# A message-passing layer with gathers on two engines: seven instead of eight one-hot tiles a pair of chunks

## The chip, the core and the metric

The kernel runs on one core of one Trainium2 chip. The metric is device time in microseconds, median of the runs; lower is better. TensorE is called PE, VectorE DVE, ScalarE ACT, GpSimd POOL and SyncE SP.

## The reference

A graph has 12500 nodes with 32 features and 400000 edges, sorted by destination. Each edge makes a value from both of its nodes and its own 32 features; each node takes the maximum over its incoming edges.

```python
h = jnp.maximum(_layernorm(x, axis=-1), 0.0)
e_feat = jnp.concatenate([h[src], h[dst], edge_attr], axis=-1)
v = jax.nn.relu(e_feat @ W1 + b1) @ W2 + b2          # (400000, 96) -> 64 -> 32
x_cand = jax.ops.segment_max(v, dst, num_segments=12500)
out = x + jnp.maximum(x_cand, h)
```

## The kernel before

The edges are cut into four stripes of 100352, and each stripe into 196 chunks of 512; a chunk `c` means 512 edges of every stripe, 2048 edges, whose 32 features times four stripes fill the 128 partitions. The main loop takes a pair of chunks a turn (`for c in range(0, NCH - 4, 2)`, with `a, b = c + 2, c + 3` the pair after the one that is being finished). 94 of its turns are alike.

The rows `h[src]` of a chunk are 16 groups of 128 edges. They come in two ways:

- **Gathered rows.** POOL issues one indirect DMA for each group of 128 rows (`gather`, line 179), three groups to a buffer `gh`. `HELD` holds some of these gathers until TensorE has reached a named point of an earlier turn (`b1` is the odd chunk's tile 1, `n0` the next even chunk's tile 0, `ea` the edge features, `ht` the gathered features, `tr` the transposes, `lv` the windows' maxima), so that POOL runs beside TensorE at a set distance.
- **Rows by matmuls, called tiles.** In chunks 2 to 193 the last `MM = 4` groups are picked out of `hs`, the whole of `h` in SBUF, by one-hot matrices (`tile`, line 344): seven slices `hot[:, k]` of 128x128 for 128 edges, each against the high and the low half of `hs`, 14 matmuls into one PSUM bank of 32 features times 14. DVE then multiplies by a mask over the 14 (`one`, line 351) and takes the maximum (line 352), which leaves one row of 32 features for each edge. In 34 of the odd chunks (`MMX`) a fifth group goes this way; its one-hots (line 274), mask and keys are made and loaded by `one_hot_x` and `load_key_x`.

The one-hots of a chunk compare `keys` (which group of 14 nodes a source belongs to) with the slice's numbers: DVE makes slices 0 to 3 in two instructions of two slices (`one_hots`, line 304), ACT slices 4 to 6 (`one_hots_act`, lines 317 and 318).

DVE turns gathered rows and tiles' rows into features by edges (`to_features`, lines 368 and 371). TensorE adds the edge features (`ea`), the destination's part (`of`, `qf`) and the gathered features (`ht`) into four banks `ph` (line 773), ACT applies the ReLU (line 798), TensorE multiplies by W2 (line 807), DVE runs a maximum along the edges (`scan`, line 815), and the last edge of each node is picked by transposes (line 669) and one-hot matmuls (line 686), for which DVE makes `last` (line 650). SP writes the windows to `top_d` (line 707).

The order on every engine is the order in which the program is written out (a manual schedule). In one turn TensorE does: `ea`, `of`, `ht`, the transposes, tiles 1 to 3 of the even chunk, the second layer, the windows' maxima, tiles 0 to 3 of the odd chunk, its fifth where there is one, and tile 0 of the next even chunk. Seven PSUM banks go round. `PAD` and its like only place buffers.

Of the kernel before, what the change touches and what calls it, by code (L numbers as in the profile page):

```python
# [8 lines left out]
F32 = mybir.dt.float32  # L9
# [15 lines left out]
P = 128  # L25
# [24 lines left out]
MMC = range(2, NCH - 2)  # L50
MMX = [17 + 2 * (k * 83 // 34) for k in range(34)]
RAW = 2
TILES = len(MMC) * MM
PLACES = TILES + len(MMX)
SLOTS = 48
PAD = 16
PAD_HOT = 24
# [19 lines left out]


def ap(t, offset, dims):
    return bass.AP(tensor=t.tensor, offset=t.offset + offset, ap=dims)  # L80


@with_exitstack
def gnn_kernel(ctx, tc, x, src, src_mm, src_x, src_t, dst, dst_ext, lo, lo_c, ends_b, edge_attr, weights, w1, w2, b2, out):

# [26 lines left out]
    top_d = dram.tile([NP, D], F32, name="top_d")  # L112
    key_d = dram.tile([(TILES + len(MMX)) * P], F16, name="key_d")
    acc_d = dram.tile([NP, D], F32, name="acc_d")
# [35 lines left out]
    place_k = const.tile([P, TILES + SLOTS], F32, name="place_k")[:, :PLACES]  # L150
    src_xi = const.tile([P, SLOTS], I32, name="src_xi")[:, :len(MMX)]
    nc.sync.dma_start(src_xi, src_x)

# [17 lines left out]


    def gather(c):
        n = min(K - MM * (c in MMC), (SE - c * C) // D) - (c in MMX)
        parts = []
        for k in range(0, n, SOME):
            parts.append(gathered.tile([P, SOME, D], F32, name="gh"))
            for i in range(min(SOME, n - k)):
                ins = nc.gpsimd.indirect_dma_start(  # L179
                    out=parts[-1][:, i, :], out_offset=None, in_=h_d[:, :],  # L180
                    in_offset=bass.IndirectOffsetOnAxis(ap=src_i[:, c, k + i:k + i + 1], axis=0))
                hold(c, k + i, ins)
        return parts
# [57 lines left out]
    def places(start, stop):  # L241

        se = src_i[:, MMC.start + start:MMC.start + stop, K - MM:]
        pk = place_k[:, :len(MMC) * MM].rearrange("p (c m) -> p c m", m=MM)[:, start:stop]
        group(pk, se)
        nc.vector.scalar_tensor_tensor(pk, pk, -float(A0), se, op0=ALU.mult, op1=ALU.add)

    extras = {}

    def places_x():  # L250

        pk = place_k[:, TILES:]
        group(pk, src_xi)
        nc.vector.scalar_tensor_tensor(pk, pk, -float(A0), src_xi, op0=ALU.mult, op1=ALU.add)

    def load_key_x(c):

        if c in MMX:
            small = early.tile([P, P // 2 + A0], F32, name="kx", bufs=2)
            key = small[:, :P // 2].bitcast(F16)  # L260
            nc.scalar.dma_start(key, ap(key_d, (TILES + MMX.index(c)) * P, [[0, P], [1, P]]))
            extras[c] = key, small[:, P // 2:], []

    def one_hot_x(c):

        if c in MMX:
            key, mask, spaces = extras[c]
            for k in range(0, A1, 2):
                if k:
                    spaces.append(early.tile([P, HALF, D], F32R, name="xg", bufs=3).rearrange("p k d -> p (k d)"))  # L270
                else:
                    spaces.append(early.tile([P, ZERO], F32R, name="zero", bufs=1)[:, :2 * P])
                n = min(2, A1 - k)
                nc.vector.tensor_tensor(spaces[-1].rearrange("p (k e) -> p k e", k=2)[:, :n],
                                        key[:, None, :].to_broadcast([P, n, P]),
                                        key_ps[:, k:k + n, None].to_broadcast([P, n, P]), op=ALU.is_equal)
            i = TILES + MMX.index(c)
            nc.vector.tensor_tensor(mask, place_ps, place_k[:, i:i + 1].to_broadcast([P, A0]), op=ALU.is_equal)

    def load_keys(c, queue=nc.scalar):  # L280

        if c in MMC and (c - MMC.start) % KEYS == 0:
            n = min(KEYS, MMC.stop - c)
            kb = early.tile([P, KEYS, MM * P], F16, name="kb", bufs=2)
            queue.dma_start(kb[:, :n], ap(key_d, (c - MMC.start) * MM * P,
                                           [[0, P], [MM * P, n], [1, MM * P]]))
            for k in range(n):
                keys[c + k] = kb[:, k]

# [7 lines left out]
    def one_hots(c, start, stop):  # L297

        if c not in MMC:
            return  # L300
        n = stop - start
        if n == 0:
            return
        nc.vector.tensor_tensor(hot_of(c)[:, start:stop], keys[c][:, None, :].to_broadcast([P, n, MM * P]),  # L304
                                key_ps[:, start:stop, None].to_broadcast([P, n, MM * P]), op=ALU.is_equal)

# [4 lines left out]
    def one_hots_act(c):  # L311

        if c not in MMC:
            return
        for k in by_act(c):
            away = early.tile([P, MM * P], F32, name="away", bufs=2)
            nc.scalar.activation(away, keys[c], AF.Square, bias=key_n[:, k:k + 1])  # L317
            nc.scalar.activation(hot_of(c)[:, k], away, AF.Relu, bias=ones, scale=-1.0)  # L318

    def mask_of(c):  # L320
        if c in MMC:
            masks[c] = early.tile([P, MM, A0], F32, name="mask", bufs=2)
            nc.vector.tensor_tensor(
                masks[c], place_ps[:, None, :].to_broadcast([P, MM, A0]),
                place_k[:, (c - MMC.start) * MM:(c - MMC.start + 1) * MM, None].to_broadcast([P, MM, A0]),
                op=ALU.is_equal)

    def tile(c, m):

        if c not in MMC or m == MM and c not in MMX:  # L330
            return
        if m == 0:
            mm_rows[c] = early.tile([P, MM, D], F32, name="gm", bufs=4)
        if m < MM:
            hot = [hots[c][:, k, m * P:(m + 1) * P] for k in range(A1)]
            mask, row = masks[c][:, m], mm_rows[c][:, m]
        else:
            _, mask, spaces = extras.pop(c)
            hot = [spaces[k // 2][:, k % 2 * P:(k % 2 + 1) * P] for k in range(A1)]
            row = gh[c][-1][:, SOME - 1]  # L340
        po = bank("pv")[:, :D * A0]
# [14 lines left out]
    def to_features(c, part):  # L356
# [6 lines left out]
        ht = hts[c]  # L363
        n = min(K - MM * (c in MMC), (SE - c * C) // D)
        if part < J:
            r = slice(part * SOME, min((part + 1) * SOME, n))
            if r.start < n:
                nc.vector.transpose(ht[:, r].rearrange("p k e -> p (k e)"),  # L368
                                    gh[c][part][:, :r.stop - r.start].rearrange("p k f -> p (k f)"))
        elif c in MMC:  # L370
            nc.vector.transpose(ht[:, n:].rearrange("p k e -> p (k e)"),
                                mm_rows.pop(c).rearrange("p k f -> p (k f)"))
        else:
            for k in range(J, len(gh[c])):
                r = slice(k * SOME, min((k + 1) * SOME, n))
                nc.vector.transpose(ht[:, r].rearrange("p k e -> p (k e)"),
                                    gh[c][k][:, :r.stop - r.start].rearrange("p k f -> p (k f)"))
# [35 lines left out]
    with tc.tile_pool(name="nodes", bufs=1) as pool, tc.tile_pool(name="nodes_ps", bufs=2, space=PSUM) as ps:  # L413
        sp = pool.tile([P, TILES + len(MMX)], I32, name="sp")
        nc.scalar.dma_start(sp, src_mm)
# [107 lines left out]
        for k in range(2):  # L523
            split_1(k)
            q_transpose(k)
        key = pool.tile([P, TILES + len(MMX)], F32, name="key")
        key16 = pool.tile([P, TILES + len(MMX)], F16, name="key16")
        group(key, sp, key16)
# [34 lines left out]
    with tc.tile_pool(name="edges", bufs=3) as pool, tc.tile_pool(name="edges_ps", bufs=1, space=PSUM) as ps:  # L563
# [290 lines left out]
        for c in range(0, NCH - 4, 2):  # L854
# [42 lines left out]
            load_keys(a + KEYS)  # L897
            load_key_x(b + 2)
            if c:
# [34 lines left out]
            if c == 2 * AHEAD:  # L934
                places(FIRST, len(MMC))
                places_x()
            if (c + 4) % BLOCK == 0 and (c + 4) // BLOCK < NB:
# [10 lines left out]
            if c:  # L948
                tile(b, 3)
            tile(b, MM)  # L950
            to_features(b, 3)
# [235 lines left out]
```

## Time and profile before

| | |
|---|---|
| median of 3 runs | 3579.48 us (3571.26 to 3581.6) |
| the profiled execution | 3575.96 us, its span 3574.1 us |
| granted TensorE clock | 0.944 |
| busy: PE, PEld, DVE, ACT, POOL | 3241.7, 2547.7, 2223.2, 1578.5, 2207.4 us |
| one-hot matmuls (line 344), busy | 2373.0 us in the largest of three groups |
| gathers (line 179) | 2291, 2169.8 us busy |

A row of a group reads: line, engine, operation, out<-in by tile names, shape, count, busy time in us and mean ns of one, and behind the second bar the idle time of the engine just ahead of these instructions, with what ended it ("issue" is a wait for nothing that the profile shows; "remote" one whose releaser it does not know). PEld is TensorE's loading of weights, which overlaps its matmuls. In a timeline a row reads: start, duration, engine, line, operation, tiles, count, and in brackets the idle time ahead. Ends of matmuls are modelled in this profile.

### The profile page before, as it was taken

To read this page: it belongs to the slowest core of one execution; us is meant where nothing else is said; L and a number is where in the kernel's file an instruction comes from. 1 tells how busy PE (TensorE), PEld (TensorE's weight loads), DVE (VectorE), ACT (ScalarE), POOL (GpSimd) and SP (SyncE) were. 2 spreads that over 40 slices of the span, in tenths; PEclk is the share of its full clock that TensorE was granted. 3 is DMA by queue.
4 is the path that set the end of the run, shared out by engine and by line. 5 is a ranking of instruction groups with operands and counts; after the bars stand their busy time and mean duration, and the time that the engine had idled before them with its cause. 6 is when DMAs were issued, how large, how long until landed. Compare 5 with 4: busy or idle time off the path is not lost.

```text
span 3574.1 us, 55458 instructions
## 1 busy us (share of the span) xinstructions
PE 3241.7 (91%) x19141; PEld 2547.7 (71%) x19141; DVE 2223.2 (62%) x4215; ACT 1578.5 (44%) x2470; POOL 2207.4 (62%) x2337
## 2 busy tenths in 40 slices
PE   5899999989999998999999999989999999999987
PEld 3577777777777776777777767777777777777765
DVE  5456666666666666666666666656665666666655
ACT  3344444443534444444443434444444444444443
POOL 6666666665666666666666666666666666666662
PEclk8899999999999999999999999999999999999997
DMA  5322222222222222222222222222222222222222
GB/s 175 99 60 62 53 64 62 62 50 62 64 62 53 61 63 65 50 66 60 62 50 70 57 56 58 59 59 61 60 62 59 60 61 61 63 65 49 59 58 65
DMA packets 178819, 227.49 MB, mean 64 GB/s; under 512 B 109621, under 2 KB 150373, under 8 KB 165734
## 3 DMA queue, kind: packets, MB, share of 16 engines
q10 hardware_dynamic: 29828, 108.01, 9.6%
q0 software_dynamic: 74336, 38.21, 8.5%
q1 hardware_dynamic: 74370, 77.70, 7.0%
q8 instruction: 151, 2.47, 0.3%
q14 instruction: 134, 1.10, 0.1%
HBM read 212.23 MB, written 11.46 MB: 63 GB/s over the span
## 4 chain that ended last, share of the span: by engine, by line
PE 81%; issue 10%; DVE 6%; another core or an unknown queue 2%; SPq 1%; DMA 1%; ACT 1%; DVEq 0%; ACTq 0%
PE pv L344 60%; PE ph L773 10%; PE pv L686 4%; PE pv L669 3%; PE pv L807 3%; DVE hot L304 1%; DVE one L351 1%; DVE last L650 1%; DVE sm L815 1%; DMA top_d<-wo 0%; DVE ht L368 0%; SPq L616 0%; SPq L707 0%; SPq L625 0%
## 5 line engine op out<-in xcount | busy, mean ns | idle before, releaser
L179 POOL DMA_INDIRECT gh<-h_d,src_i x2291 | 2169.8, 947 | 1296.3 <-issue 560.0
L344 PE MATMUL pv<-hs,hot 128*128 128x448 f32 x10752 | 2373.0, 378 | 97.5 <-issue 83.9
L344 PEld LDWEIGHTS pv<-hs,hot 128*128 128x128 f32 x10752 | 2089.1, 196 | 345.7 <-issue 159.7
L351 DVE TENSOR_TENSOR one<-pv,mask 128x448 f32<-128x448 f32 x768 | 472.3, 615 | 1219.7 <-remote 464.7
L798 ACT ACTIVATE hid<-ph,wt 128x512 f32<-128x512 f32 x392 | 250.0, 688 | 1124.6 <-remote 498.2
L352 DVE TENSOR_REDUCE gm<-one 128x32 f32<-128x448 f32 x768 | 476.2, 620 | 26.5
L304 DVE TENSOR_TENSOR hot<-kb,consts 128x1024 fp32r<-128x1024 f16 (+1 forms) x379 | 447.5, 1199 | 0.0
L318 ACT ACTIVATE hot<-away,ones 128x512 fp32r<-128x512 f32 x582 | 421.6, 724 | 45.0 <-remote 26.1
L317 ACT ACTIVATE away<-kb,key_n 128x512 f32<-128x512 f16 x582 | 416.0, 715 | 0.0
L692 ACT ACTIVATE wo<-pv 128x256 f32<-128x256 f32 x95 | 36.6, 385 | 631.2 <-remote 439.2
L815 DVE TENSOR_TENSOR_SCAN sm<-pb,sm,pv 128x512 f32<-128x512 bf16 x195 | 243.6, 1249 | 16.5 <-remote 9.0
L686 PEld LDWEIGHTS pv<-so,last 128*128 128x128 f32 x768 | 107.5, 191 | 159.5 <-issue 148.5
L773 PE MATMUL ph<-ht,wt 32*64 32x512 f32 x1568 | 197.3, 618 | 21.0 <-issue 13.0
L686 PE MATMUL pv<-so,last 128*128 128x256 f32 x768 | 148.6, 304 | 74.3 <-issue 67.7
L368 DVE STREAM_TRANSPOSE ht<-gh 128x96 f32<-128x96 f32 x774 | 207.4, 269 | 1.2
L661 ACT ACTIVATE sb<-sm,wt 128x512 f32<-128x512 f32 x196 | 138.1, 715 | 138.7 <-issue 87.6
L669 PEld LDWEIGHTS pv<-ident,sb 128*128 128x128 f32 x782 | 91.8, 150 | 120.3 <-issue 95.1
L773 PE MATMUL ph<-of,qf 32*64 32x512 f32 x1552 | 147.6, 600 | 19.6 <-issue 17.5
L669 PE MATMUL pv<-ident,sb 128*128 128x128 f32 x782 | 126.4, 298 | 30.4 <-issue 24.4
L773 PEld LDWEIGHTS ph<-ht,wt 32*64 32x64 f32 x1568 | 62.7, 135 | 114.1 <-issue 98.5
L642 ACT ACTIVATE of<-of,ones 128x512 f32<-128x512 f32 x194 | 140.6, 725 | 6.3
L641 ACT ACTIVATE of<-db,below 128x512 f32<-128x512 int32 x194 | 137.4, 708 | 0.0
(115 smaller groups left out, 1328.2 us busy)
## 6 DMA issues: line engine op xcount, KB each, us to landing
ea<-in_edge_attr SPq DMA_DIRECT2D x49, 1024.0 KB
db<-in_dst_ext ACTq DMA_DIRECT2D x48, 1024.0 KB
gh<-h_d,src_i POOLq DMA_INDIRECT x2291
pb<-pen_d ACTq DMA_DIRECT2D x48, 512.0 KB
kb<-key_d ACTq DMA_DIRECT2D x47, 512.0 KB
top_d<-wo SPq DMA_DIRECT2D x752, 3.0 KB
qf<-q_d SPq DMA_DIRECT2D x392, 16.0 KB
q_d<-qs SPq DMA_DIRECT2D x6, 512.0 KB
```

What stands on the lines that cost most here:

```text
L179: ins = nc.gpsimd.indirect_dma_start(out=parts[-1][:, i, :], out_offset=None, in_=h_d[:, :], in_offset=bass.IndirectOffsetOnAxis(ap=src_i[ ...
L304: nc.vector.tensor_tensor(hot_of(c)[:, start:stop], keys[c][:, None, :].to_broadcast([P, n, MM * P]), key_ps[:, start:stop, None].to_broad ...
L317: nc.scalar.activation(away, keys[c], AF.Square, bias=key_n[:, k:k + 1])
L318: nc.scalar.activation(hot_of(c)[:, k], away, AF.Relu, bias=ones, scale=-1.0)
L344: ins = nc.tensor.matmul(po, hot[k], hs[:, part, k].rearrange("p f a -> p (f a)"), start=(k == 0 and part == 0), stop=(k == A1 - 1 and par ...
L351: nc.vector.tensor_tensor(one, of_group, mask[:, None, :].to_broadcast([P, D, A0]), op=ALU.mult)
L352: nc.vector.tensor_reduce(row, one, axis=AX.X, op=ALU.max)
L669: passes(c // 2 + 1, "tr", nc.tensor.transpose(px[:, j, :], sb[:, j * P:(j + 1) * P], ident))
L686: ins = nc.tensor.matmul(pw[:, x % n], last[x][:, j].rearrange("p s w -> p (s w)"), sos[x][0][:, j], start=(j == 0 and x < n), stop=(j == ...
L773: ins = nc.tensor.matmul(ph[s][x * HID:(x + 1) * HID], w[g], e[g], start=start, stop=stop)
L798: nc.scalar.activation(hid[k], of, AF.Relu, bias=b1c)
L815: nc.vector.tensor_tensor_scan(found[:, :n], loaded.pop(c)[2][:, :n], pv[:, :n], -LOW if before is None else before[:, C - 1:C], op0=ALU.a ...
```

## The change

Even chunks keep four tiles; odd chunks have three, and the fifths of 34 odd chunks are gone, so a pair has seven tiles. Odd chunks gather 13 groups instead of 12 or 11; their last buffer holds four groups (`gl`, two buffers), and the buffers of three are 13 instead of 14. The fifths' keys, one-hots, masks and loads go. The one-hots, masks and keys of odd chunks shrink to three groups. `HELD` is written anew for 25 gathers a pair, with 11 points instead of 12 (there is no `b3` any more).

```diff
-MMX = [17 + 2 * (k * 83 // 34) for k in range(34)]
...
-HELD = {0: (3, 'b1'), 2: (3, 'b2'), 4: (3, 'b3'), 6: (3, 'n0'), 8: (2, 'ea'), 10: (2, 'ht'), 12: (2, 'tr'), 14: (2, 'a1'), 16: (2, 'a2'), 18: (2, 'a3'), 20: (2, 'lv'), 22: (2, 'b0')}
+HELD = {0: (3, 'b1'), 2: (3, 'b2'), 5: (3, 'n0'), 8: (2, 'ea'), 10: (2, 'ht'), 12: (2, 'tr'), 14: (2, 'a1'), 16: (2, 'a2'), 19: (2, 'a3'), 22: (2, 'lv'), 24: (2, 'b0')}
...
+def tiles_of(c):
+    return MM - c % 2 if c in MMC else 0
...
-    gathered = ctx.enter_context(tc.tile_pool(name="gathered", bufs=14))
+    gathered = ctx.enter_context(tc.tile_pool(name="gathered", bufs=13))
...
+    def rows_in(c):
+
+        n = min(K - tiles_of(c), (SE - c * C) // D)
+        at = list(range(0, n, SOME)) + [n]
+        if len(at) > 2 and at[-1] - at[-2] == 1:
+            del at[-2]
+        return [slice(k, m) for k, m in zip(at, at[1:])]
+
     def gather(c):
-        n = min(K - MM * (c in MMC), (SE - c * C) // D) - (c in MMX)
         parts = []
-        for k in range(0, n, SOME):
-            parts.append(gathered.tile([P, SOME, D], F32, name="gh"))
-            for i in range(min(SOME, n - k)):
+        for r in rows_in(c):
+            if r.stop - r.start > SOME:
+                parts.append(gathered.tile([P, SOME + 1, D], F32, name="gl", bufs=2))
+            else:
+                parts.append(gathered.tile([P, SOME, D], F32, name="gh"))
...
-        nc.vector.tensor_tensor(hot_of(c)[:, start:stop], keys[c][:, None, :].to_broadcast([P, n, MM * P]),
-                                key_ps[:, start:stop, None].to_broadcast([P, n, MM * P]), op=ALU.is_equal)
+        w = tiles_of(c) * P
+        nc.vector.tensor_tensor(hot_of(c)[:, start:stop, :w], keys[c][:, None, :].to_broadcast([P, n, w]),
+                                key_ps[:, start:stop, None].to_broadcast([P, n, w]), op=ALU.is_equal)
...
-        if c not in MMC or m == MM and c not in MMX:
+        if m >= tiles_of(c):
             return
...
-            load_key_x(b + 2)
...
-            one_hot_x(b)
...
-            tile(b, MM)
```

On TensorE, one turn of the main loop with a fifth tile, from the edge features on, stood in this order before (L344 are tiles; `zero` and `xg` hold the fifth's one-hots):

```order
L773 MATMUL ph<-ea,wt 64x512 x8
L773 MATMUL ph<-of,qf 64x512 x8
L773 MATMUL ph<-ht,wt 64x512 x8
L669 MATMUL pv<-ident,sb 128x128 x8
L344 MATMUL pv<-hs,hot 128x448 x42
L807 MATMUL pv<-hid,wt 32x512 x8
L686 MATMUL pv<-so,last 128x256 x8
L344 MATMUL pv<-hs,hot 128x448 x56
L344 MATMUL pv<-hs,zero 128x448 x4
L344 MATMUL pv<-hs,xg 128x448 x10
L344 MATMUL pv<-hs,hot 128x448 x14
```

The same turn now, with line numbers of the changed kernel:

```order
L758 MATMUL ph<-ea,wt 64x512 x8
L758 MATMUL ph<-of,qf 64x512 x8
L758 MATMUL ph<-ht,wt 64x512 x8
L654 MATMUL pv<-ident,sb 128x128 x8
L328 MATMUL pv<-hs,hot 128x448 x42
L792 MATMUL pv<-hid,wt 32x512 x8
L671 MATMUL pv<-so,last 128x256 x8
L328 MATMUL pv<-hs,hot 128x448 x56
```

Between the windows' maxima (`so`, `last`) and the next edge features stood six tiles, or five in a turn without a fifth; now there are four (56 matmuls), three of the odd chunk and the next even chunk's first.

On DVE, the part of a turn from the odd chunk's second tile to its third stood so before, in a turn with a fifth tile (`hot` is the second half of DVE's one-hots of the next even chunk):

```order
L351 TENSOR_TENSOR one<-pv,mask 128x448
L352 TENSOR_REDUCE gm<-one 128x32
L368 STREAM_TRANSPOSE ht<-gh 128x96
L650 TENSOR_TENSOR last<-consts,at 128x512 x2
L304 TENSOR_TENSOR hot<-kb,consts 128x1024
L323 TENSOR_TENSOR mask<-consts,place_k 128x56
L274 TENSOR_TENSOR zero<-kx,consts 128x256
L274 TENSOR_TENSOR xg<-kx,consts 128x256 x2
L274 TENSOR_TENSOR xg<-kx,consts 128x128
L278 TENSOR_TENSOR kx<-consts,place_k 128x14
```

It now stands so, and runs on to the end of the odd chunk:

```order
L335 TENSOR_TENSOR one<-pv,mask 128x448
L336 TENSOR_REDUCE gm<-one 128x32
L353 STREAM_TRANSPOSE ht<-gh 128x96
L635 TENSOR_TENSOR last<-consts,at 128x512 x2
L291 TENSOR_TENSOR hot<-kb,consts 128x1024
L312 TENSOR_TENSOR mask<-consts,place_k 128x56
L335 TENSOR_TENSOR one<-pv,mask 128x448
L336 TENSOR_REDUCE gm<-one 128x32
L353 STREAM_TRANSPOSE ht<-gh 128x96
L353 STREAM_TRANSPOSE ht<-gl 128x128
L356 STREAM_TRANSPOSE ht<-gm 128x96
```

The fifth's five instructions are gone from behind the mask. What stands ahead of the one-hots is the same as before; the odd chunk's third tile is now its last, and its last gathered buffer has four groups.

More of the change, by code (lines that the diff above doesn't have):

```diff
@@ L50 @@
 MMC = range(2, NCH - 2)
-MMX = [17 + 2 * (k * 83 // 34) for k in range(34)]
 RAW = 2
[L53 to L56, printed above, removed]
+TILES = sum(MM - c % 2 for c in MMC)
+PAD = 48
 PAD_HOT = 24
@@ L76, with first_of @@
 EPS = 1e-5
+def tiles_of(c):
+    return MM - c % 2 if c in MMC else 0
+def first_of(c):
+    return sum(tiles_of(k) for k in range(MMC.start, c))
 def ap(t, offset, dims):
@@ L112, in gnn_kernel @@
     top_d = dram.tile([NP, D], F32, name="top_d")
-    key_d = dram.tile([(TILES + len(MMX)) * P], F16, name="key_d")
+    key_d = dram.tile([TILES * P], F16, name="key_d")
     acc_d = dram.tile([NP, D], F32, name="acc_d")
@@ L170, in gnn_kernel @@
     general_i = const.tile([1, 1], I32, name="general_i")
+    def rows_in(c):
[4 more added lines that the diff above has]
+        return [slice(k, m) for k, m in zip(at, at[1:])]
     def gather(c):
-        n = min(K - MM * (c in MMC), (SE - c * C) // D) - (c in MMX)
         parts = []
-        for k in range(0, n, SOME):
-            parts.append(gathered.tile([P, SOME, D], F32, name="gh"))
-            for i in range(min(SOME, n - k)):
+        for r in rows_in(c):
[3 more added lines that the diff above has]
+                parts.append(gathered.tile([P, SOME, D], F32, name="gh"))
+            k = r.start
+            for i in range(r.stop - r.start):
                 ins = nc.gpsimd.indirect_dma_start(
@@ L241, in places @@
     def places(start, stop):
[L243 to L278, printed above, removed]
+        pairs = place_k.rearrange("p (c m) -> p c m", m=2 * MM - 1)[:, start // 2:stop // 2]
+        for x in range(2):
+            n = MM - x
+            se = src_i[:, MMC.start:MMC.stop].rearrange("p (c x) t -> p c x t", x=2)[:, start // 2:stop // 2, x, K - n:]
+            pk = pairs[:, :, x * MM:x * MM + n]
+            group(pk, se)
+            nc.vector.scalar_tensor_tensor(pk, pk, -float(A0), se, op0=ALU.mult, op1=ALU.add)
     def load_keys(c, queue=nc.scalar):
@@ L284, in load_keys @@
             kb = early.tile([P, KEYS, MM * P], F16, name="kb", bufs=2)
-            queue.dma_start(kb[:, :n], ap(key_d, (c - MMC.start) * MM * P,
-                                           [[0, P], [MM * P, n], [1, MM * P]]))
+            flat = kb.rearrange("p k e -> p (k e)")
+            at = [(first_of(k) - first_of(c)) * P for k in range(c, c + n + 1)]
+            queue.dma_start(flat[:, :at[n]], ap(key_d, first_of(c) * P, [[0, P], [1, at[n]]]))
             for k in range(n):
-                keys[c + k] = kb[:, k]
+                keys[c + k] = flat[:, at[k]:at[k + 1]]
     def hot_of(c):
@@ L333, in tile @@
             mm_rows[c] = early.tile([P, MM, D], F32, name="gm", bufs=4)
[L334 to L340, printed above, removed]
+        hot = [hots[c][:, k, m * P:(m + 1) * P] for k in range(A1)]
+        mask, row = masks[c][:, m], mm_rows[c][:, m]
         po = bank("pv")[:, :D * A0]
@@ L363, in to_features @@
         ht = hts[c]
-        n = min(K - MM * (c in MMC), (SE - c * C) // D)
+        rows = rows_in(c)
+        n = rows[-1].stop
         if part < J:
-            r = slice(part * SOME, min((part + 1) * SOME, n))
-            if r.start < n:
+            if part < len(rows):
+                r = rows[part]
                 nc.vector.transpose(ht[:, r].rearrange("p k e -> p (k e)"),
@@ L371, in to_features @@
             nc.vector.transpose(ht[:, n:].rearrange("p k e -> p (k e)"),
-                                mm_rows.pop(c).rearrange("p k f -> p (k f)"))
+                                mm_rows.pop(c)[:, :K - n].rearrange("p k f -> p (k f)"))
         else:
             for k in range(J, len(gh[c])):
-                r = slice(k * SOME, min((k + 1) * SOME, n))
+                r = rows[k]
                 nc.vector.transpose(ht[:, r].rearrange("p k e -> p (k e)"),
@@ L525, in gnn_kernel @@
             q_transpose(k)
-        key = pool.tile([P, TILES + len(MMX)], F32, name="key")
-        key16 = pool.tile([P, TILES + len(MMX)], F16, name="key16")
+        key = pool.tile([P, TILES], F32, name="key")
+        key16 = pool.tile([P, TILES], F16, name="key16")
         group(key, sp, key16)
@@ L1143 @@
     sc = np.ascontiguousarray(sp.reshape(NS, NCH, K, D).transpose(1, 2, 0, 3).reshape(NCH, K, P))
-    sm = np.concatenate([sc[MMC.start:MMC.stop, K - MM:].reshape(-1),
-                         sc[MMX, K - MM - 1].reshape(-1)])
+    sm = np.concatenate([sc[c, K - tiles_of(c):].reshape(-1) for c in MMC])
     w1, w2 = np.asarray(L0_gnn_W1), np.asarray(L0_gnn_W2)
```

22 lines of the change are left out of this document (10 added, 12 removed).

## The prediction

> **What bounds the kernel now.** I read the page first, for the busy times and the chain of work that ended last.
>
> ```profile
> span 3574.1 us, 55458 instructions
> PE 3241.7 (91%) x19141; PEld 2547.7 (71%) x19141; DVE 2223.2 (62%) x4215; ACT 1578.5 (44%) x2470; POOL 2207.4 (62%) x2337
> PE 81%; issue 10%; DVE 6%; another core or an unknown queue 2%; SPq 1%; DMA 1%; ACT 1%; DVEq 0%; ACTq 0%
> ```
>
> TensorE is busy for 91% of the span and carries 81% of the chain. Next I read the groups by line with shapes kept apart, for what TensorE does in its time and what the rows of this change cost.
>
> ```profile
> L344 PE MATMUL pv<-hs,hot 128*128 128x448 f32 x10752 | 2373.0, 378 | 97.5 <-issue 83.9 <-DVE hot L304 7.8 <-ACT qs L505 1.1
> L179 POOL DMA_INDIRECT gh<-h_d,src_i x2291 | 2169.8, 947 | 1296.3 <-issue 560.0 <-remote 289.8 <-PE pv L344 238.8
> L368 DVE STREAM_TRANSPOSE ht<-gh 128x96 f32<-128x96 f32 x773 | 207.2, 269 | 1.2
> L344 PE MATMUL pv<-hs,xg 128*128 128x448 f32 x340 | 85.2, 404 | 0.0
> L344 PE MATMUL pv<-hs,zero 128*128 128x448 f32 x136 | 37.4, 399 | 41.7 <-DVE zero L274 27.1 <-issue 7.0 <-DVE hot L304 4.4
> ```
>
> The one-hot matmuls of line 344 are 2373.0 + 85.2 + 37.4 = 2496 us of TensorE's 3242. POOL, which gathers the other rows, was idle for 1296 us ahead of its gathers, and DVE, which turns the gathered rows, was idle 1.2 us in all ahead of line 368: rows from gathers are always there in time. So the kernel is bound by TensorE, and POOL has slack. The change moves work from the first to the second. The question is how far POOL's slack reaches, and what the removed matmuls had been hiding.
>
> **TensorE's part.** There are (10752 + 340 + 136) / 14 = 802 tiles now: 192 chunks of four and 34 fifths. After, there are 96 pairs of seven, 672. 130 tiles go, 96 of them the odd chunk's fourth and 34 the fifths. For the price of a fourth I take one undisturbed stretch of the timeline of TensorE, in a pair without a fifth tile. It shows the second layer, the windows' maxima, and then the odd chunk's four tiles with the next chunk's first as one run:
>
> ```profile
> 1721.11 1.09 PE L807 MATMUL pv<-hid,wt 64*32 64x512 f32 x16
> 1722.12 1.38 PE L686 MATMUL pv<-so,last 128*128 128x256 f32 x8
> 1723.34 14.62 PE L344 MATMUL pv<-hs,hot 128*128 128x448 f32 x70
> 1737.89 1.11 PE L773 MATMUL ph<-ea,wt 32*64 32x512 f32 x16
> ```
>
> Seventy matmuls in 14.62 us are 0.209 us each, 2.92 us a tile. 96 x 2.92 = 281 us. The fifths go with their own two groups, 85.2 + 37.4 = 123 us, and with the 41.7 us that TensorE stood ahead of them. Together 281 + 123 + 42 = 446 us of TensorE's time, all of it on the path: -446. (The group's mean, 2373.0 / 10752 = 0.2207, would make the fourths 297, 16 us more; it also holds half-speed stretches that the fourths seldom stand in.)
>
> **POOL's part.** 130 rows of 128 are gathered instead: 2291 + 130 = 2421 gathers. The timeline of POOL shows its pace where nothing holds it:
>
> ```profile
> 53.18 0.94 POOL L179 DMA_INDIRECT gh<-h_d,src_i  x1 [0.30 <-issue]
> ...
> 2000.24 0.95 POOL L179 DMA_INDIRECT gh<-h_d,src_i  x1 [0.30 <-issue]
> 2001.49 0.95 POOL L179 DMA_INDIRECT gh<-h_d,src_i  x1 [0.30 <-issue]
> ...
> 2018.26 0.94 POOL L179 DMA_INDIRECT gh<-h_d,src_i  x1 [0.30 <-issue]
> 2028.86 0.95 POOL L179 DMA_INDIRECT gh<-h_d,src_i  x1 [4.65 <-PE pv L344]
> ...
> 3518.05 0.95 POOL L179 DMA_INDIRECT gh<-h_d,src_i  x1 [0.30 <-issue]
> ```
>
> One gather starts 1.25 us after the other. Of the 1296 us of idle time, 2291 x 0.30 = 687 are that pace and 609 are waits, mostly the holds on TensorE's progress (the row at 2028.86). 130 x 1.25 = 163 us fit into 609, so this costs nothing while POOL has the slack. A pair now needs 25 x 1.25 = 31.25 us of POOL. That makes a floor: the first gather of this line starts at 53.18, and 56 us of the span follow the start of the last one at 3518.05. If both ends stay, POOL alone needs 53 + 2421 x 1.25 + 56 = 3135 us.
>
> TensorE without the 130 tiles would end at 3576 - 446 = 3130, practically the same. Both engines would be full, so neither can pay for a wait of the other any more. POOL's holds (11 now, at gathers 0, 2, 5, 8 ...) bind only where POOL is ahead.
>
> **What the removed tiles covered.** This is the step that decides. DVE makes slices 2 and 3 of the next even chunk's one-hots late in the pair. In program order they stand behind the odd chunk's second tile; TensorE needs them in the next chunk's first tile, from its fifth matmul on (two per slice). DVE's timeline in the same pair:
>
> ```profile
> 1730.75 0.62 DVE L351 TENSOR_TENSOR one<-pv,mask 128x448 f32<-128x448 f32 x1 [0.66 <-PE pv L344]
> 1731.41 0.62 DVE L352 TENSOR_REDUCE gm<-one 128x32 f32<-128x448 f32 x1
> 1731.94 0.27 DVE L368 STREAM_TRANSPOSE ht<-gh 128x96 f32<-128x96 f32 x1
> 1732.14 1.25 DVE L650 TENSOR_TENSOR last<-consts,at 128x512 fp32r<-128x512 f32 x2
> 1733.31 1.21 DVE L304 TENSOR_TENSOR hot<-kb,consts 128x1024 fp32r<-128x1024 f16 x1
> ```
>
> The one-hots are ready at 1733.31 + 1.21 = 1734.52. TensorE's run started at 1723.34, so by its rows the odd chunk's tiles end at 1726.3, 1729.2, 1732.1 and 1735.0, and the fifth matmul of the next tile stands at 1735.0 + 0.8 = 1735.8: ready 1.3 us early. Without the fourth tile it stands at 1732.9, and the one-hots are 1.6 us late. Nothing ahead of them on DVE moves forward; only work behind them goes. TensorE, stalled there, has the whole next pair queued behind it. The bounds: DVE saw the second tile done at 1730.75, not at 1729.2, so the array may run 1.5 us behind these rows; then the stall is about 0.1 us. If the rows are exact, it is 1.6 us, and more in pairs where DVE runs later. The nearest row is a wait of the same kind at the same place, TensorE waiting for the fifth's one-hots, which DVE makes right behind these: 41.7 us of idle time ahead of 34 tiles, 1.2 us each. I take 1.2: 96 x 1.2 = +115, with ends of 10 and 154.
>
> Such a wait has a second price. The table of stretches shows one of those 34 waits and what came behind it (columns: length, busy time of PE, PEld, DVE, ACT, POOL, granted clock, DMA share, GB/s):
>
> ```profile
> 1587.80:1591.20 3.40, 0.72 (x4) 0.70 (x5) 3.40 (x9) 0.07 (x1) 2.64 (x3) 1.00 0.45 62
> 1591.20:1594.60 3.40, 3.40 (x11) 3.01 (x10) 2.54 (x6) 0.00 (x0) 1.89 (x2) 0.51 0.41 78
> ...
> 1590.48 1.19 PE L344 MATMUL pv<-hs,zero 128*128 128x448 f32 x4 [2.79 <-DVE zero L274]
> ```
>
> After 2.79 us of waiting the granted clock was 0.51 for the next stretch, 11 matmuls in 3.40 us where 16 would fit at 0.209: 1.1 us, up to 1.7 where the stretch is full of work. At a mean of 1.2 us most waits are too short for that. I take one in three at 1.6 us: 96 / 3 x 1.6 = +51; the ends are 0 and 96 x 1.7 = 163. [...]
>
> **Edits at nothing.** The fifths' one-hots on DVE (line 274) and key loads go; DVE is busy 62% and SP and ACT issue less. The odd chunk's one-hots shrink by a quarter on DVE and ACT. The fourth tile's mask and maximum go. A buffer of four rows and 13 in place of 14 buffers of three hold 47 rows, not 42. SP's queue keeps its order. DVE's work could pull the late one-hots forward a little; that lies inside the bounds.
>
> **The sum.** The profiled execution took 3575.96 us, 0.1% under the median 3579.48; 2 us lie around its span. 3576 - 446 + 115 + 51 = 3296; I say 3300.
>
> **Rivals.** *Nothing stalls:* the one-hots arrive in time because the array is behind its rows. Then TensorE's 3130 and POOL's 3135 meet, and jitter adds a little: 3135 to 3180. For it speaks the 1730.75 above, against it the 41.7 us of waits in spite of two tiles of cover.
>
> *The stall trips the clock in every pair:* 1.6 us and 1.7 us in each, 96 x 3.3 = 317, so 3130 + 317 = 3447. For it speaks the row at 0.51, against it that the mean wait is under half of 2.79.
>
> *Slower, by POOL's holds:* if POOL's 609 us of waits are not slack but each hold sits in a ring (POOL waits for a TensorE mark, DVE for POOL's rows, TensorE for DVE), they stay as gathers come on top: 3135 + 609 = 3744. It decides from the point at which DVE begins to wait ahead of line 368; today 1.2 us in all speak against it.
>
> **How the numbers follow.** The forecast (3230 to 3400) has 0.55, no stall 0.17, the clock in every pair 0.16, POOL's ring 0.10, and 0.02 for mixtures that end where the kernel is now. The first and third and half of the second make 0.8: the range is 3165 to 3470. Faster by over 0.3%, about what a measurement of this kernel can tell, is 0.88, within it 0.02, slower 0.10.
>
> **What would show it.** Right: 9408 matmuls of the one-hot line with about 2060 us busy; 2421 gathers with 1.25 us between starts and their waits down from 609 us to some 250; a new wait of TensorE for DVE's one-hots (the even chunk's, 128x1024), about 1 us in most pairs; still no wait of DVE ahead of the gathered rows' transposes. Wrong: gathers with as much idle time as before, DVE waiting for gathers, a pair that takes 35 us or more, or a granted clock well under 0.94.

## The result, and the profile after

The changed kernel takes 3745.1 us, the median of four runs (3731.07 to 3757.09), beside 3575.37 of the kernel before: a ratio of 1.0474, 95% interval 1.0425 to 1.0523. It is slower, where 3300 was forecast. The first two rows of its page, of an execution of 3757.09 us with a granted clock of 0.891:

```profile
span 3755.3 us, 51651 instructions
PE 3056.6 (81%) x17321; PEld 2289.8 (61%) x17321; DVE 1974.9 (53%) x3788; ACT 1511.5 (40%) x2470; POOL 2324.3 (62%) x2467
```

TensorE has 1820 matmuls fewer and 185 us less busy time, but the span grew by 181 us. The groups by line with shapes kept apart, for TensorE's tiles, POOL's gathers and DVE's turning of gathered rows (line 328 was 344, 193 was 179, 353 was 368):

```profile
L328 PE MATMUL pv<-hs,hot 128*128 128x448 f32 x9408 | 2284.9, 399 | 489.8 <-issue 340.2 <-DVE hot L291 144.1 <-ACT away L305 1.1
L193 POOL DMA_INDIRECT gh<-h_d,src_i x2033 | 1921.0, 945 | 1150.8 <-issue 502.0 <-remote 279.0 <-PE pv L328 228.2
L193 POOL DMA_INDIRECT gl<-h_d,src_i x388 | 366.0, 943 | 200.4 <-issue 94.2 <-remote 67.8 <-PE pv L328 29.1
L353 DVE STREAM_TRANSPOSE ht<-gh 128x96 f32<-128x96 f32 x677 | 181.2, 268 | 0.0
```

The tiles stand 489.8 us behind idle time where they had 97.5, and 144.1 of it is put down to DVE's one-hots, which had 7.8. POOL was idle for 1150.8 + 200.4 = 1351 us ahead of 2421 gathers; 2421 x 0.30 = 726 are its pace, so 625 are waits, as many as before (609). DVE never waited for a gathered row (0.0). So in this profile POOL does not set the time. The larger part of the 489.8 us (340.2) is put down to nothing ("issue"); the timelines show what it is. TensorE's timeline in one pair, from the windows' maxima to the next edge features:

```profile
2033.19 1.22 PE L671 MATMUL pv<-so,last 128*128 128x256 f32 x8
2034.25 9.89 PE L328 MATMUL pv<-hs,hot 128*128 128x448 f32 x46
2049.12 3.83 PE L328 MATMUL pv<-hs,hot 128*128 128x448 f32 x10 [4.98 <-issue]
2052.88 1.11 PE L758 MATMUL ph<-ea,wt 32*64 32x512 f32 x16
```

46 matmuls are the odd chunk's three tiles and the first four of the next even chunk's first tile. Ahead of the fifth TensorE stands for 4.98 us: the place that the prediction named. The other ten take 3.83 us, not the 2.1 that they need at 0.209. DVE's timeline there:

```profile
2042.45 0.62 DVE L335 TENSOR_TENSOR one<-pv,mask 128x448 f32<-128x448 f32 x1 [5.95 <-remote]
...
2045.31 0.61 DVE L335 TENSOR_TENSOR one<-pv,mask 128x448 f32<-128x448 f32 x1
...
2046.69 1.25 DVE L635 TENSOR_TENSOR last<-consts,at 128x512 fp32r<-128x512 f32 x2
2047.86 1.21 DVE L291 TENSOR_TENSOR hot<-kb,consts 128x1024 fp32r<-128x1024 f16 x1
```

The one-hots are ready at 2049.07 and TensorE goes on at 2049.12. It is so in nearly every pair: in 86 of 87 this fifth matmul starts within 0.1 us of the end of the one-hots, after a mean wait of 3.36 us. So TensorE waits for one-hots, "issue" or not. DVE is late here because it began the odd chunk's first tile at 2042.45, after 5.95 us of waiting, though by TensorE's rows that tile ended near 2034.25 + 14 x 0.209 = 2037.2. The table of stretches shows the clock behind the wait (columns as in the prediction):

```profile
2046.20:2049.60 3.40, 0.48 (x2) 0.46 (x3) 3.40 (x7) 2.30 (x4) 2.56 (x3) 0.98 0.18 23
2049.60:2053.00 3.40, 3.40 (x17) 2.54 (x24) 1.29 (x6) 0.00 (x0) 0.27 (x1) 0.52 0.31 71
```

The next table is worked out from TensorE's timeline: mean us a pair over 87 pairs, from the first matmul of a block to the first of the next one. Its two right-hand columns are profiles of later runs, which the next section brings in.

| block | before, recorded | after, recorded | before, later run | after, later run |
|---|---|---|---|---|
| odd chunk's fourth tile and fifth | 4.65 | 0 | 4.02 | 0 |
| next even chunk's first tile | 3.10 | 7.55 | 2.98 | 3.44 |
| gathered features (`ht`) | 1.93 | 2.44 | 0.99 | 5.18 |
| the whole pair | 35.77 | 37.63 | 30.19 | 31.26 |
| of it at half clock | 3.18 | 7.61 | 0.00 | 3.85 |

In the recorded pair of profiles 4.65 us went and 4.45 came back at the next even chunk's first tile; the rest (+2.06) is spread over the other blocks. Half-clock time grew by 4.43 us a pair, 3.05 of it in that tile.

### The profile page after: what moved, and what is told of

It is laid out like the page before. It is cut to its first block, busy times and chain, and to the rows that moved or that the text cites. A ratio compares the mean times of both kernels' runs of the same rounds, so it can differ in the third digit from the quotient of the medians.

```text
span 3755.3 us, 51651 instructions
## 1 busy us (share of the span) xinstructions
PE 3056.6 (81%) x17321; PEld 2289.8 (61%) x17321; DVE 1974.9 (53%) x3788; ACT 1511.5 (40%) x2470; POOL 2324.3 (62%) x2467
## 5 line engine op out<-in xcount | busy, mean ns | idle before, releaser
L328 PE MATMUL pv<-hs,hot 128*128 128x448 f32 x9408 | 2284.9, 399 | 489.8 <-issue 340.2
L193 POOL DMA_INDIRECT gh<-h_d,src_i x2033 | 1921.0, 945 | 1150.8 <-issue 502.0
L328 PEld LDWEIGHTS pv<-hs,hot 128*128 128x128 f32 x9408 | 1925.8, 208 | 805.2 <-issue 478.8
L335 DVE TENSOR_TENSOR one<-pv,mask 128x448 f32<-128x448 f32 x672 | 415.6, 618 | 1631.7 <-remote 667.6
L193 POOL DMA_INDIRECT gl<-h_d,src_i x388 | 366.0, 943 | 200.4 <-issue 94.2
L336 DVE TENSOR_REDUCE gm<-one 128x32 f32<-128x448 f32 x672 | 416.7, 620 | 23.1
L306 ACT ACTIVATE hot<-away,ones 128x512 fp32r<-128x512 f32 (+1 forms) x582 | 390.2, 671 | 29.9 <-remote 11.0
L291 DVE TENSOR_TENSOR hot<-kb,consts 128x768 fp32r<-128x768 f16 (+2 forms) x379 | 396.9, 1066 | 0.0
L305 ACT ACTIVATE away<-kb,key_n 128x512 f32<-128x512 f16 (+1 forms) x582 | 384.8, 661 | 0.0
L353 DVE STREAM_TRANSPOSE ht<-gh 128x96 f32<-128x96 f32 x678 | 181.4, 268 | 0.0
```

The lines of the kernel that those rows point to most:

```text
L193: ins = nc.gpsimd.indirect_dma_start(out=parts[-1][:, i, :], out_offset=None, in_=h_d[:, :], in_offset=bass.IndirectOffsetOnAxis(ap=src_i[ ...
L291: nc.vector.tensor_tensor(hot_of(c)[:, start:stop, :w], keys[c][:, None, :].to_broadcast([P, n, w]), key_ps[:, start:stop, None].to_broadc ...
L305: nc.scalar.activation(away[:, :w], keys[c], AF.Square, bias=key_n[:, k:k + 1])
L306: nc.scalar.activation(hot_of(c)[:, k, :w], away[:, :w], AF.Relu, bias=ones, scale=-1.0)
L328: ins = nc.tensor.matmul(po, hot[k], hs[:, part, k].rearrange("p f a -> p (f a)"), start=(k == 0 and part == 0), stop=(k == A1 - 1 and par ...
L335: nc.vector.tensor_tensor(one, of_group, mask[:, None, :].to_broadcast([P, D, A0]), op=ALU.mult)
```

## The experiments

All ran on chips 14, 0, 1, 3 and 9. There the kernel before takes 3005 us (medians 3004.55 to 3006.27), not 3575, and no later run took 3575. The record doesn't name the chip of the recorded executions, so whether that was a sixth chip or one of these at another time is not known. Expectations in absolute time that count from 3575 or 3745 can't be held against these runs; what tells is how the kernels of one chip stand to each other.

**The changed kernel again** (no edit), on chip 0.

> The changed kernel itself, beside the kernel before on the same chip. POOL's pace as the floor: where the kernel before takes about 3005 us, this takes 3100 (50 + 2421 x 1.25 + 22), ratio 1.032, with gathers 1.25 us apart and hardly a wait of POOL. Late one-hots as the cause on every chip: it takes the kernel before's time and some 170 us more, ratio 1.047, with the 7.5 us stretch from the odd chunk's last tile to the next even chunk's first in every pair, as in the recorded profile.

It took 3101.09 us beside 3006.06, ratio 1.0322 [1.0305, 1.0339]: POOL's floor. The first rows of the two pages, first of the kernel before (a run of its own, 3004.6 us), then of the changed one:

> The kernel before, for its profile on a chip where it takes about 3005 us, if it is one of those. POOL's pace: POOL has little slack even here, 50 + 2291 x 1.25 + 22 = 2936 of 3005, so its waits are some 70 us, not 609, and TensorE is busy for 97% or more. Late one-hots as the cause: TensorE waits for DVE's one-hots for under 30 us, as in the recorded profile.

```profile
span 3002.5 us, 55458 instructions
PE 2937.1 (98%) x19141; PEld 2392.5 (80%) x19141; DVE 2232.7 (74%) x4215; ACT 1566.2 (52%) x2470; POOL 2201.5 (73%) x2337
```

```profile
span 3099.1 us, 51651 instructions
PE 2717.7 (88%) x17321; PEld 2114.7 (68%) x17321; DVE 1990.4 (64%) x3788; ACT 1502.2 (48%) x2470; POOL 2325.4 (75%) x2467
```

The groups of the kernel before there:

```profile
L179 POOL DMA_INDIRECT gh<-h_d,src_i x2291 | 2163.5, 944 | 739.8 <-issue 471.9 <-DMA gh<-h_d,src_i 90.2 <-PE pv L344 76.6
L368 DVE STREAM_TRANSPOSE ht<-gh 128x96 f32<-128x96 f32 x773 | 207.7, 269 | 19.5 <-DMA gh<-h_d,src_i 18.3
```

And of the changed kernel there:

```profile
L758 PE MATMUL ph<-ht,wt 32*64 32x512 f32 x1568 | 204.2, 803 | 299.4 <-DVE ht L356 299.4
L193 POOL DMA_INDIRECT gh<-h_d,src_i x2033 | 1920.9, 945 | 622.9 <-issue 361.8 <-DMA gh<-h_d,src_i 149.4 <-DMA gl<-h_d,src_i 19.2
L193 POOL DMA_INDIRECT gl<-h_d,src_i x388 | 366.6, 945 | 118.2 <-issue 64.9 <-DMA gh<-h_d,src_i 40.2 <-PE pv L328 5.2
L353 DVE STREAM_TRANSPOSE ht<-gh 128x96 f32<-128x96 f32 x677 | 183.3, 271 | 249.9 <-DMA gh<-h_d,src_i 249.2
L353 DVE STREAM_TRANSPOSE ht<-gl 128x128 f32<-128x128 f32 x96 | 28.7, 298 | 357.9 <-DMA gl<-h_d,src_i 304.7 <-DMA gh<-h_d,src_i 53.0
```

In the kernel before POOL was idle for 739.8 us, and 2291 x 0.30 = 687 are its pace: 53 us of waits, not 609. In the changed kernel 622.9 + 118.2 - 726 = 15 are left, DVE waits 249.9 + 357.9 us for gathered rows, and TensorE for DVE's features. The first and the last gather, and one of TensorE's waits, by the timelines:

```profile
49.57 0.94 POOL L193 DMA_INDIRECT gh<-h_d,src_i  x1 [0.30 <-issue]
...
3077.06 0.94 POOL L193 DMA_INDIRECT gh<-h_d,src_i  x1 [0.30 <-issue]
```

```profile
2050.26 1.02 PE L758 MATMUL ph<-ht,wt 32*64 32x512 f32 x2
2059.24 2.00 PE L758 MATMUL ph<-ht,wt 32*64 32x512 f32 x14 [7.96 <-DVE ht L356]
```

(3077.06 - 49.57) / 2420 = 1.251 us a gather over the whole program, and 22 us of the span follow the last start. A pair needs 25 x 1.25 = 31.25 us of POOL and takes 31.26. POOL is the bound.

**The one-hots early.** All four of DVE's slices are made behind the even chunk's last rows, ahead of the odd chunk's tiles.

```diff
-                one_hots(a + 2, 0, 2)
+                one_hots(a + 2, 0, by_act(a + 2).start)
...
-                one_hots(a + 2, 2, by_act(a + 2).start)
```

> The changed kernel, with DVE's four one-hot slices of the next even chunk made at once where the first two stand now (behind the even chunk's last tile), not the second two behind the odd chunk's second tile. Late one-hots: the next chunk's first tile, 7.55 us in the changed kernel's turns against 3.1 before, falls to about 3 us and the clock comes back above 0.94; the time falls by 95 x 4.4 = 420 us or more, to 3150 to 3350 us. POOL's ring: nothing that POOL or its holds wait for has moved, so it stays at 3745, within 1%.

**No holds** on POOL's gathers.

```diff
-        at = HELD.get(i + c % 2 * (K - MM))
+        at = None
```

> The changed kernel without POOL's holds on TensorE's progress (its buffers and the few early holds stay). Late one-hots: TensorE still waits for DVE's one-hots, 3745 within 2%. POOL's ring: the 625 us of waits of POOL go and the time with them, to 3150 to 3300 us.

**A cover in the removed tile's place:** 14 matmuls into a spare bank, whose result nobody reads.

```diff
                 tile(b, 3)
+            if c and a + 2 < NCH - 2:
+                spare = bank("pv")[:, :D * A0]
+                for k in range(A1):
+                    for part in range(2):
+                        nc.tensor.matmul(spare, hots[b][:, k, :P], hs[:, part, k].rearrange("p f a -> p (f a)"),
+                                         start=(k == 0 and part == 0), stop=(k == A1 - 1 and part == 1))
```

> The changed kernel, with 14 matmuls of no use put between the odd chunk's last tile and the next even chunk's first, into a PSUM bank that nobody reads: the cover of the removed fourth tile without its row. Late one-hots: the 2.9 us a turn fill a wait that is there anyway and keep the clock up, so the time does not rise and rather falls, to 3550 to 3745 us. TensorE's own load or POOL's ring: 95 x 2.9 = 275 us more, 4020, or no change at most.

The three took 3102.0, 3100.69 and 3101.19 us beside 3004.89 on one chip, ratios 1.0326 [1.0309, 1.0344], 1.032 [1.0303, 1.0337] and 1.0324 [1.0307, 1.0341]. Three different edits change nothing, and the changed kernel itself takes 3101.09. The cover's 94 tiles of 2.89 us, 272 us of matmuls, were free: TensorE had that much room under POOL's pace. Without holds POOL gains nothing, so they are no ring here. The first of the three was run again on chips 0 and 9, with 3102.26 and 3100.92 us:

> The changed kernel with DVE's four slices of the next even chunk's one-hots made at once, behind the even chunk's last rows. POOL's pace: 3100 where the kernel before takes 3005, the same as the changed kernel within 0.2%; where the kernel before takes 3575 and POOL has slack, no change that matters. Late one-hots: where the kernel before takes 3575, it falls from 3745 to 3300 to 3450, since the wait ahead of the next even chunk's first tile goes and with it the half clock behind it.

> The changed kernel with DVE's four slices of the next even chunk's one-hots made at once, behind the even chunk's last rows. Where the kernel before takes 3575: 3745 less up to 96 x 4.45 = 430, 3315 to 3450, if the recorded wait ahead of the next even chunk's first tile is the loss; 3700 or more if the loss lies elsewhere. Where the kernel before takes 3005: 3100, POOL's pace.

**24 gathers a pair.** One gather of each odd chunk is left out and an older row is turned in its place; TensorE's work stays.

```diff
-            for i in range(r.stop - r.start):
+            skip = c in MMC and r.stop - r.start > SOME
+            for i in [i for i in range(r.stop - r.start) if not (skip and i == 2)]:
...
```

> The changed kernel with one gather less in each odd chunk of the main part (24 a pair, 2325 in all); DVE turns an older row in its place, so the features of that group are left out, and nothing changes on TensorE. POOL's pace: 96 x 1.25 = 120 us less, 50 + 2325 x 1.25 + 22 = 2978, where the kernel before takes 3005, until TensorE's own time ends it (2880 to 2980 by the page of the variant with all one-hots early). Late one-hots: no change against the changed kernel (3100 or 3745), since no one-hot comes earlier.

2981.01 us beside 3101.09 of the changed kernel on the same chip: 120 us for 96 gathers, 1.25 each, and 3 us from the floor's 2978. This shows the bound: the time follows POOL's count.

**18 gathers a pair, and no holds,** to see TensorE's own time with seven tiles:

```diff
-        for r in rows_in(c):
+        for r in rows_in(c)[:3 if c in MMC else None]:
...
-        at = HELD.get(i + c % 2 * (K - MM))
+        at = None
...
```

> The changed kernel without the last buffer of gathered rows of each chunk of the main part (18 gathers a pair, 1749 in all; DVE turns older rows in their place, so those groups' features are left out) and without holds. POOL's floor is then 50 + 1749 x 1.25 + 22 = 2258, and what is left is TensorE's own time with seven tiles. POOL's pace as the only bound of the changed kernel: 3005 - 96 x 2.89 - 34 x 3 = 2626, and some 45 more for the one-hots that come late: about 2670, where the kernel before takes 3005; where it takes 3575 and POOL has slack, no change against 3745. Late one-hots as the larger cause: 3000 or more even so.

The same with the one-hots early (the diff above):

> The same, and all four of DVE's slices of the next even chunk's one-hots made behind the even chunk's last rows. It prices the wait for the one-hots alone, with POOL out of the way: 96 x 0.47 = 45 us under the run with 18 gathers where the kernel before takes 3005 (2626), 96 x 4.45 = 430 us under it where that takes 3575, if the late one-hots and the half clock behind them are what the recorded profile shows. If one-hots have no part: the same as with 18 gathers.

2657.86 and 2616.62 us beside 3005.49. The late one-hots cost 41 us, 0.43 a pair. The removed matmuls are worth 3005.49 - 2616.62 = 389 us of TensorE's time, 4.05 a pair. The waits of the first of the two (us, times, longest) show the stall itself, small and in nearly every pair:

```profile
PEld pv L328 <- DVE hot L291: 48.4, 93, 0.5
```

In the profile of the kernel before (chip 1) the same one-hots are ready 2.65 us ahead of TensorE's fifth matmul in a turn without a fifth tile; here that matmul stands 0.30 us late. The difference is about one tile (2.89 us).

A second run of the other one, on chip 9, took 2614.65:

> The same with 18 gathers a pair and no holds. Where the kernel before takes 3575: the same as the run before this one within 2%, if POOL has slack there; 100 us or more under it if POOL's gathers or holds take part. Where the kernel before takes 3005: 2617, TensorE's own time.

**DVE made late.** The four matrices `last` of a pair are made three times over in the same place, which was to be 2.5 us more just ahead of the late one-hots and came to 2.4 (the row of line 639 below, 3.64 us for six, less 1.25 for two): with eight tiles, with seven (18 gathers), and with seven and the one-hots early.

```diff
             last = [lasts(c + x) for x in range(2)]
+            for x in (0, 1, 0, 1):
+                lasts(c + x, last[x])
```

> The kernel before, and 2.5 us of DVE work more a pair just ahead of the late one-hots (the four matrices of line 650 are made three times over, into the same place). The removed tile as cover: the next even chunk's first tile stands 2.9 us later than with seven tiles, where the one-hots were 0.4 us late, so they are 2.5 us early and the delay is covered: 3005 to 3035. If it is not covered: 3005 + 96 x 2.5 = 3245.

> The changed kernel with 18 gathers a pair and without holds, and the same 2.5 us of DVE work more ahead of the late one-hots. The removed tile as cover: nothing covers the delay now, TensorE waits 0.4 + 2.5 us in every pair, 2658 + 96 x 2.5 = 2898, and if a wait of 2.9 us trips the clock as the recorded profile has it, up to 1.7 us more a pair: 3060. A granted clock of 0.94 or less would be the mark of that. If the tile covered nothing: 2658 to 2690.

> The same 2.5 us of DVE work at the same place, with all four of DVE's slices of the next even chunk's one-hots made earlier, so that they no longer stand behind it. The removed tile as cover: 2617 to 2660, the delay meets nothing that TensorE waits for. If DVE's delay costs by another way than the one-hots (banks, rows): about as much as in the run before this one, 2850 or more.

With eight tiles: 3058.4 us, 54 more than before, where 30 at most were expected; by the timelines the next even chunk's first tile takes 2.95 us, as it did (2.98), and 34.6 of the 54 us are a wait that the kernel before didn't have there, for the fifths' one-hots, which DVE also makes behind the delay (why the other 19 us were lost stays open):

```profile
L344 PE MATMUL pv<-hs,zero 128*128 128x448 f32 x136 | 35.8, 385 | 34.6 <-DVE zero L274 34.6
```

With seven tiles: 2990.24, 332 more than without the delay, 3.46 a pair for 2.4 us of DVE. With the one-hots early: 2645.08, 28 more. So the removed tile was the cover, and the one-hots are the way. TensorE's and DVE's timelines of the run with seven tiles, one place:

```profile
1499.82 2.84 PE L328 MATMUL pv<-hs,hot 128*128 128x448 f32 x13
1505.19 3.66 PE L328 MATMUL pv<-hs,hot 128*128 128x448 f32 x10 [2.54 <-DVE hot L291]
1508.79 1.25 PE L762 MATMUL ph<-ea,wt 32*64 32x512 f32 x16
```

```profile
1500.37 3.64 DVE L639 TENSOR_TENSOR last<-consts,at 128x512 fp32r<-128x512 f32 x6
1503.93 1.20 DVE L291 TENSOR_TENSOR hot<-kb,consts 128x1024 fp32r<-128x1024 f16 x1
```

And its table of stretches there:

```profile
1502.10:1505.50 3.40, 0.86 (x5) 0.48 (x3) 3.40 (x7) 0.11 (x1) 2.31 (x3) 1.00 0.40 65
1505.50:1508.90 3.40, 3.40 (x18) 2.59 (x24) 3.23 (x11) 0.00 (x0) 0.00 (x0) 0.53 0.40 79
```

This is the recorded picture made on purpose: a wait ahead of the fifth matmul, then a stretch at 0.53 with ten matmuls in 3.66 us. The run's granted clock is 0.949 where the same kernel without the delay has 0.989; 2.66 us a pair are at half clock.

**Fewer fifths in the kernel before,** one and 18 instead of 34.

```diff
-MMX = [17 + 2 * (k * 83 // 34) for k in range(34)]
+MMX = [17]
```

```diff
+MMX = [17 + 2 * (k * 83 // 18) for k in range(18)]
```

> The kernel before with one fifth tile in place of 34 (33 more groups gathered). If tiles are plain load on a full TensorE: 33 x 2.9 plus most of the 42 us ahead of them go, 3435 to 3450 us. If a fifth tile gives DVE the time that the next turn needs, as the turns right behind one with a fifth (32.8 us against 36.2) suggest: 94 turns of about 36.2 us, 3580 to 3620 us.

> The kernel before with 18 odd chunks with a fifth tile, not 34: 2307 gathers, 16 x 14 matmuls fewer. POOL's pace: 50 + 2307 x 1.25 + 22 = 2956, and TensorE 3005 - 16 x 3 = 2957 where the kernel before takes 3005: about 2960, ratio 0.985, under both the kernel before and the one with one fifth (2983). Late one-hots: no bearing, 16 x 3.5 = 56 us less than the kernel before, 2949, and 3519 where that takes 3575.

2983.29 beside 3004.89, ratio 0.9929 [0.9913, 0.9946], and 2960.55 beside 3006.06, ratio 0.9851 [0.9835, 0.9868]. With one fifth POOL's floor sets the time (50 + 2324 x 1.25 + 22 = 2977); with 34 it is TensorE. 18 stand where both meet: of the versions run that compute the whole result the fastest, 1.5% under the kernel before. Its page, the busy times and the chain of waits:

```profile
PE 2893.5 (98%) x18917; PEld 2353.2 (79%) x18917; DVE 2193.1 (74%) x4103; ACT 1565.4 (53%) x2470; POOL 2217.0 (75%) x2353
PE 91%; DMA 5%; DVE 1%; POOL 1%; issue 1%; ACT 0%; SPq 0%; ACTq 0%; POOLq 0%; DVEq 0%
```

## Why the prediction was wrong

**What bounds the kernel: half right.** TensorE was the bound and POOL had slack in the recorded profile. But the 609 us of POOL's waits were taken as room in the program. In the later profile of the same program (chip 1) POOL's waits are 53 us. The 609 came with some 570 us by which the recorded execution took longer; they belonged to it and not to the schedule.

**TensorE's part, -446, "all of it on the path": right for the fourth tiles, wrong for the fifths in the recorded profile.** A fourth tile had held 2.84 us there and 2.89 later, as taken. But by TensorE's timeline of the recorded kernel before, in the same 87 pairs, the 34 turns with a fifth take 38.57 us and the turns right behind them 32.80, 71.37 us for the two; two of the 19 other turns take 71.58 (single turns of a kind scatter by about 1 us). What a fifth cost came back in the next turn, so the 123 + 42 us for the fifths were worth about nothing: 165 us, or 1.7 of the 2.06 us a pair by which the other blocks grew in the mean. In the later profile nothing comes back: 31.95 us with a fifth, 29.06 behind it and elsewhere, and there the removed tiles are worth 389 us. The busy time of the tiles came out at 2284.9 us, not 2060; where hardly any stretch is at half clock (18 gathers a pair) it is 1981.6.

**POOL's floor, 3135: right as a mechanism, and the bound in the later runs.** The pace of 1.25 us held, and nearly the start (49.57 for 53.18); the tail was 22 us, not 56, so 3100. The prediction set both engines equal at 3130 and saw that neither could pay for the other. Against a kernel before of 3005 the same floor means slower by 3.2%.

**The stall at the next even chunk's first tile, +115 and +51: right in place and kind, wrong in size; in the recorded profile this is the step that failed most.** It came to 4.45 us a pair, 427 us, where 166 were allowed and 317 in the rival in which the clock trips in every pair. The 1.2 us of the first price was drawn from waits for the fifths' one-hots, which had two tiles of cover; the lateness itself had been worked out for one pair only (1.6 us). The same working for all 87 pairs of the same trace (when the one-hots are ready, less the start of the fourth tile's fifth matmul) gives 2.38 us a pair, 228 us. The wait then measured was 3.36 us. DVE starts on the odd chunk's second tile 3.19 us after TensorE's rows of it end, where it was 2.10 before (means over the 87 pairs), and from there to the end of the one-hots it takes 3.76 us in both. So the 1.5 us by which the prediction saw DVE behind these rows, and which it read as relief ("the array may run behind these rows"), is part of the stall. Why this lateness grew by 1.1 us is open. The run with DVE made late shows the cost on its own: for 2.4 us of DVE past the cover, TensorE's wait for the one-hots (by its weight loads) goes from 48.4 to 270.7 us in 93 waits, 2.39 us each, and with the half clock behind it the pair grows by 3.46 us. In the later runs, where DVE starts 0.04 us after TensorE's rows end, the stall is 0.43 us, a third of what was taken.

**The second price: mis-sized with it.** One pair in three was allowed a slow stretch of 1.6 us, 0.53 us a pair; the ten matmuls behind the wait take 3.37 us in the mean where 2.1 would do, 1.27 us a pair. The run with DVE made late shows the same: its waits of 2.54 us go with 2.66 us a pair at half clock.

Together the stall (261 us over what was allowed) and the fifths (165 us) account for 426 of the 445 us between 3300 and 3745.

**The rival "Slower, by POOL's holds" gave 3744, and 3745 was measured, by chance.** Its condition, DVE waiting ahead of the gathered rows, did not come (0.0 us), and taking the holds away changes nothing where POOL binds. Without holds no run met the recorded conditions. POOL's unchanged waits there fit TensorE's longer pair: 37.63 - 31.25 = 6.38 us a pair, 612 us of the 625.

**Its own signs.** Of the right ones, 2421 gathers 1.25 us apart, a wait for the 128x1024 one-hots and no wait of DVE came; 2060 us and waits of 250 did not. Three signs against it came: as much idle time of POOL, a pair over 35 us (37.63), a clock of 0.891.

**What stays open.** Why the recorded executions take 3575 us for what takes 3005 on five chips later, with the same counts and DVE and POOL instructions of the same length (`hot` 1194 ns in both, gathers 947 and 944). What differs is that results of TensorE reach DVE later than TensorE's rows end, at the odd chunk's first two tiles by up to 4.3 us in the recorded kernel before and 8.2 in the changed one; ends of matmuls are modelled, so whether the work or the signal is late can't be read. That a fifth tile gives its time back to the next turn there is measured, but not why. And that the one-hots made early would bring the 427 us back under those conditions is argued from the run with DVE made late, not shown: no run met them.

## What to carry to other kernels

Before work is moved from the engine that binds to one with slack, work out the receiver's own floor (count times pace, and both ends) and hold it against the donor's own busy time a turn, not against the span: idle time of the receiver may belong to the run and not to the program. When a tile of work is taken out, look for what is produced beside it and used right behind it, and work out the producer's lateness for every turn of the trace, not for one. When what goes stands in some turns only, compare those turns and the ones behind them with the others: its own time is not yet what it costs. Then balance the two engines by counts: here 18 fifth tiles were better than 34 and than one.

## What the runs showed of the hardware

One program took 3005 us on five chips (medians within 0.1%) and 3575 in the recorded executions, with other waits ruling in its profile, so one trace says less of a program's slack than it seems to. In the run with DVE made late TensorE waited 236.0 us for the one-hots, 2.54 in the mean of 93 waits, and 2.66 us a pair were at half clock (0.53 in the 3.40 us behind one such wait); with 18 gathers and no delay the longest of these waits was 0.5 us, and 0.00 us a pair were at half clock. Which waits lower the clock the runs did not show: in the recorded kernel before, the 3.40 us behind a wait of 1.83 us (at 2021.15) had a granted clock of 0.53, those behind one of 2.70 us (at 3166.61) had 1.00. 2421 indirect gathers of 128 rows from POOL kept 1.251 us each through a whole program: a floor that no edit elsewhere moved (3100.69 to 3102.26 us).
